# A four-layer graph network on one core: two groups' recurrences in alternate steps, and states brought back to rows by block turns and DRAM

## The chip, the cores and the metric

The kernel runs on one NeuronCore of one Trainium2 chip. The metric is device time in microseconds (us) of one launch. The time before is the median of three runs, 1408.24 us (1407.55 to 1408.32).

## What is computed

The input is `x` (128 graphs, 64 nodes, 256 features, float32) with an adjacency `adj` (128, 64, 64) of zeros and ones. Four layers follow each other; each takes `h = relu(layernorm(x))` and adds its result to `x`:

- layer 0: graph attention with four heads of 64 features; layer 1: graph attention with one head of 256 features;
- layer 2: a relational convolution; since `adj` holds only 0 and 1, only its loop relation counts;
- layer 3: a gated recurrence of three steps, which is where the change lies:

```python
for i in range(3):
    m = jnp.einsum('bnd,de->bne', h, weight[i])
    aggr = jnp.einsum('bst,bsd->btd', A, m)      # A = (adj != 0)
    gi, gh = aggr @ w_ih.T + b_ih, h @ w_hh.T + b_hh
    r, z = sigmoid(i_r + h_r), sigmoid(i_z + h_z)
    n = tanh(i_n + r * h_n)
    h = (1 - z) * n + z * h
```

## The kernel before

**Groups.** The 8192 node rows are cut into 16 groups of 512 rows (8 graphs, `G = 4` tiles of 128 rows). For each group the kernel runs layers 0 to 2 and then the recurrence. All matmuls are float32, and one product in the program is two passes in the trace (a transpose is one).

**How the order comes about.** The program does not issue its instructions as it is written. The class `Plan` notes every operation with the engine, a cost, the tiles it touches and a due time (`begin(name, start, end)`), then lays all of them on the five engines in its own model of time, and emits them in that order (`forward`, `backward`, `emit`, L316 to L472). Every engine then works through a fixed list, in order. The due times are constants in the last part of the program: `start, period = 87.96, 83.9` places the recurrence of group `g` at `start + g * period`, and layers 0 to 2 of later groups are placed ahead of it, so that their work fills the recurrence's waits. Since nearly all noted operations go through one helper, they all carry its line, L485; the small products of `beside` carry L706.

**One step of the recurrence** (`recurrence`, from L855). A state lives turned, as `hT` (features on partitions, 512 nodes along). A step has two chunks of 128 output features (`Chunk`). A chunk forms the gates r and z by a seven-product scheme (`mul`, products 1 to 7, with sums of states `hS`, `aS` made on GpSimd by `state_sums`) in the PSUM tiles `ry`, `rm`, `rz`, and the candidate in `nh`, `ni`. ScalarE copies the partial sums out of `ry` three times per chunk while it is still being added to; VectorE and ScalarE do the gates; the last two VectorE operations (`h_there`) write the new `hT`.

**The sum over neighbours** (`along`) needs the state as rows, `hnat` (nodes on partitions). It multiplies 64 by 64 blocks, four at a time in the four quarters of the array (`beside`, L706), into PSUM tiles `tp` and `tq`, from which ScalarE writes `aT`. The rows come from `back`: four TensorE transposes per 128 features into `tp`, and a ScalarE copy to `hnat`, or, after the third step, a VectorE addition of `x`. So a step has eight transposes. In the second and third steps `along` is issued in two halves, one per 128 features, so that the first can begin before the second chunk of the state is there:

```python
along(psum, hnat, abd, aT, [0])      # 16 products 64x64, then state_sums(aT, aS, 0)
...
back(hT, hnat, 1)                    # 4 transposes and a copy
along(psum, hnat, abd, aT, [1])
```

**Groups in time.** The three steps of one group follow each other directly, and then come the three of the next: a step's first products need the state that the step before has just finished.

**PSUM.** [...] `Banks` gives one each to `ry`, `rm`, `rz`, `nh` and `ni`, and three (`mt`) to everything else. **Transfers.** All but the first few DMAs are issued from one queue, that of SyncE (SP), in the planned order; from group 2 on, layers 0 to 2 and the start of the recurrence turn their input by a VectorE block turn (`nc.vector.transpose`, 32 by 32 blocks) and 16 small DMAs (`hT<-hn`) that move the blocks to their places (`layernorm_T_by_dma`).

Of the kernel before, what the change touches and what calls it, by code (L numbers as in the profile page):

```python
# [195 lines left out]
class Op:  # L196
    def __init__(self, engine, call, cost, port, dma, job, number):
        self.engine, self.call, self.cost, self.port, self.dma = engine, call, cost, port, dma
        self.job, self.number = job, number
        self.after, self.then, self.bases, self.needs = {}, [], [], []  # L200

# [18 lines left out]
class Plan:  # L220
# [60 lines left out]
    ISSUE = 665.0  # L281
# [34 lines left out]
    def forward(self):  # L316
# [11 lines left out]
        wire = 2500.0  # L328
# [29 lines left out]
        while len(order) < len(self.ops):  # L358
# [31 lines left out]
            if op.dma:  # L390
                wire = max(wire, t + 1350.0) + op.cost
                op.end = wire + 400.0
            else:
                took = op.cost
                if op.port:
                    other = "Pool" if e == "DVE" else "DVE"
                    took = max(took, held[other] + min(op.port, took) - t)
                    held[e] = t + took
                op.end = t + took + (165.0 if e == "PE" else 0.0)
                free[e] = t + took - (op.cost - op.busy)  # L400
# [118 lines left out]
def cost(engine, method, args, kwargs):  # L519

    n = elements(args[0])
    if engine == "tensor":
        m = elements(args[2] if method == "matmul" else args[0])
        return max(m / 1.2, 118.0) * (1 if method == "transpose" else 2)
# [17 lines left out]
def kernel(  # L542
# [62 lines left out]

    def pair(hT, k, s):
# [3 lines left out]
    def layernorm_T(work, psum, src, hT, natural=None, graphs=False):  # L610
# [28 lines left out]
        if natural is not None:  # L639
            nc.vector.tensor_scalar(natural, hn, 0.0, None, op0=ALU.max)  # L640

    def layernorm_T_by_dma(work, src, hT, natural=None, graphs=False):
# [14 lines left out]
        for p in range(n):  # L657
            nc.scalar.activation(hn[:, p, :], src[:, p, :], AF.Relu, bias=var[:, p : p + 1], scale=rstd[:, p : p + 1])
        tb = work.tile([P, K, n, P], F32, name="tb")
        nc.vector.transpose(tb.rearrange("p k n q -> p n k q"), hn.rearrange("p n (k q) -> p n k q", k=K))  # L660
# [10 lines left out]
    def transpose_blocks(psum, dst, src, rblocks, scale=1.0):  # L671

        for k in range(K):
            for r0 in range(0, rblocks, 4):
# [4 lines left out]
                nc.scalar.mul(dst[:, k, r0 * P : (r0 + n) * P], pt[:, : n * P], scale)  # L679
# [20 lines left out]
    def beside(products, cost):  # L700
# [10 lines left out]
        nc.note("PE", emit, cost, [Plan.all_of(x) for x in writes], [x for p in products for x in p[1:]])  # L711
# [61 lines left out]
    def aggregate_graphs(work, psum, t, wv, heads, by_scalar=False):  # L773
# [5 lines left out]
        for u in range(n // 2):  # L779
# [8 lines left out]
            beside(products, 710.0 if heads > 1 else 660.0)  # L788
# [11 lines left out]
    def along(psum, hnat, abd, aT, cs):  # L800
# [3 lines left out]
        for i, c in enumerate(cs):  # L804
            for p in range(G):
                for half, ps in enumerate(banks):
                    b = slice(half * N, (half + 1) * N)
                    for f in range(0, P, N):
                        products.append((ps[f : f + N, i, p, :], hnat[b, p, c * P + f : c * P + f + N], abd[b, p, :]))
        beside(products, 230.0 + 480.0 * len(cs))  # L810
# [29 lines left out]
    def before_recurrence(work, psum, src, adjacency, abd, by_dma=False):  # L840

        hT = work.tile([P, K, T], F32, name="hT")
        hnat = work.tile([P, G, D], F32, name="hnat")
# [5 lines left out]
        aT = work.tile([P, K, T], F32, name="aT")  # L849
        along(psum, hnat, abd, aT, range(K))  # L850
        hS = work.tile([P, 4, T // 2], F32, name="hS")
        aS = work.tile([P, 4, T // 2], F32, name="aS")
        for k in range(K):
            state_sums(hT, hS, k)
            state_sums(aT, aS, k)  # L855
        return hT, aT, hS, aS

    def recurrence(work, psum, start, src, abd, store, in_parts=False):

        hT, aT, hS, aS = start  # L860

        def back(hT, hnat, c, plus=None, p0=0, n=G):

            pt = psum.tile([P, n, P], F32, name="tp")
            for p in range(n):
                nc.tensor.transpose(pt[:, p, :], hT[:, c, (p0 + p) * P : (p0 + p + 1) * P], ident)
            part = (slice(None), slice(p0, p0 + n), slice(c * P, (c + 1) * P))
            if plus is None:
                nc.scalar.copy(hnat[part], pt)
            else:  # L870
                nc.vector.tensor_tensor(hnat[part], pt, plus[part], ALU.add)
                if in_parts:
                    store(hnat, part)

        class Chunk:
# [3 lines left out]
            def __init__(self, c, i, hT, hnew):  # L879
                self.c, self.i, self.hT, self.hnew = c, i, hT, hnew  # L880
                self.banks, self.started = {}, set()
                self.r, self.t, self.z, self.d = (work.tile([P, T], F32, name=name) for name in "rtzd")

            def bank(self, name):

                if name in self.banks:
                    return self.banks[name], False
                self.banks[name] = psum.tile([P, T], F32, name=name)
                return self.banks[name], True

            def mul(self, name, q, source):

                w, m, ms = ((whh, self.hT, hS), (wc[:, self.i], aT, aS))[source]
                ws = wsum[:, (0, 1 + self.i)[source]]
                cs = slice(self.c * P, (self.c + 1) * P)
                zs = slice(D + self.c * P, D + (self.c + 1) * P)
                lhsT, rhs = {
                    1: (w[:, 0, cs], m[:, 0, S0]),
                    2: (w[:, 1, cs], m[:, 1, S0]),
                    3: (ws[:, 2, cs], m[:, 1, S1]),  # L900
                    4: (w[:, 1, zs], ms[:, 3]),
                    5: (ws[:, 0, cs], ms[:, 0]),
                    6: (ws[:, 1, cs], ms[:, 1]),
                    7: (w[:, 0, zs], ms[:, 2]),
                }[q]
                ps, new = self.bank(name)
                nc.tensor.matmul(
                    ps[:, S0], lhsT, rhs, start=new, stop=(source == 1 and q in (2, 3, 4)), skip_group_check=True
                )
                return 0.43  # L910

            def both(self, name, q):
                return self.mul(name, q, 0) + self.mul(name, q, 1)

            def gate(self, name, k):

                w, m = {"nh": (whh, self.hT), "ni": (wc[:, self.i], aT)}[name]
                ps, new = self.bank(name)
                f = 2 * D + self.c * P
                nc.tensor.matmul(ps, w[:, k, f : f + P], m[:, k, :], start=new, stop=not new)  # L920
                return 0.86

            def nh_there(self):
                nc.scalar.activation(self.t, self.banks["nh"], AF.Identity, bias=bh[:, 4 + self.c : 5 + self.c])

            def r_there(self, h):

                r, t = self.r[:, h], self.t[:, h]
                if h == S0:
                    nc.vector.tensor_tensor(r, self.banks["rm"][:, S0], r, ALU.add)  # L930
                    y = r
                else:
                    y = self.banks["ry"][:, S0]
                nc.scalar.activation(r, y, AF.Tanh, bias=brz[:, self.c : self.c + 1], scale=0.5)
                nc.vector.scalar_tensor_tensor(t, r, 1.0, t, op0=ALU.add, op1=ALU.mult)

            def n_there(self, h):
                t = self.t[:, h]
                nc.vector.tensor_tensor(t, t, self.banks["ni"][:, h], ALU.add)
                nc.scalar.activation(t, t, AF.Tanh, bias=bi[:, 4 + self.c : 5 + self.c])  # L940
                nc.gpsimd.tensor_tensor(self.d[:, h], self.hT[:, self.c, h], t, ALU.subtract)

            def m1_there(self):
                nc.scalar.copy(self.r[:, S0], self.banks["ry"][:, S0])

            def m16_there(self):
                nc.scalar.copy(self.z[:, S0], self.banks["ry"][:, S0])

            def m165_there(self):
                nc.scalar.copy(self.z[:, S1], self.banks["ry"][:, S0])  # L950

            def z_there(self, h):

                z = self.z[:, h]
                nc.vector.tensor_tensor(z, self.banks["rz"][:, S0], z, ALU.add)
                nc.scalar.activation(z, z, AF.Tanh, bias=brz[:, 2 + self.c : 3 + self.c], scale=0.5)

            def h_there(self, h):
                d = self.d[:, h]
                nc.vector.scalar_tensor_tensor(d, self.z[:, h], 1.0, d, op0=ALU.add, op1=ALU.mult)  # L960
                nc.vector.scalar_tensor_tensor(
                    self.hnew[:, self.c, h], d, 0.5, self.t[:, h], op0=ALU.mult, op1=ALU.add
                )

        for i in range(LAYERS):
            last = i == LAYERS - 1
# [5 lines left out]
            if i > 0:  # L972
                aT = work.tile([P, K, T], F32, name="aT")
                if 0:
                    back(hT, hnat, 1)
                    along(psum, hnat, abd, aT, range(K))
                else:
                    along(psum, hnat, abd, aT, [0])
                state_sums(aT, aS, 0)
# [3 lines left out]
            if i > 0 and not 0:  # L983
                back(hT, hnat, 1)
            a.gate("nh", 1)
            a.nh_there()
            if i > 0:
                if not 0:
                    along(psum, hnat, abd, aT, [1])
                state_sums(aT, aS, 1)  # L990
# [34 lines left out]
            hnat = work.tile([P, G, D], F32, name="hnat")  # L1025
            back(hnew, hnat, 0, src if last else None)
# [618 lines left out]
```

## Time and profile before

| what | us |
|---|---|
| median of three runs | 1408.24 |
| the profiled execution's own time | 1407.86 |
| its span, first to last instruction | 1406.1 |
| TensorE (PE) busy | 1390.5 |
| VectorE (DVE) busy | 1026.9 |
| ScalarE (ACT) busy | 811.0 |
| GpSimd (POOL) busy | 609.7 |

The profile is of one execution. A group's "busy" is the time in which at least one of its instructions was running; for matmuls the ends are modelled and overlap, so the pitch, from the start of one to the start of the next, is what a product takes of TensorE. In a timeline line the columns are the start and the duration in us, engine, line, operation, output<-inputs, the part of the array used, shape and count; what stands in brackets at the end is idle time and what ended it.

### The profile page before, as it was taken

The numbers are of one execution on the slowest core, as the hardware profiler recorded it, in microseconds if no ns is written. First come the engines' busy times: TensorE is split into PE (matmuls) and PEld (weight loads), VectorE is DVE, ScalarE is ACT, GpSimd is POOL, SyncE is SP. The second block draws the span as 40 slices with busy tenths as digits, with TensorE's granted clock in tenths as the row PEclk, the third lists the DMA queues.
The fourth block names the chain that finished last, engine by engine and source line by source line (L and its number), as shares of the span: only waits on it lengthen the run. The fifth ranks groups of instructions, "written<-read, shape, count | busy, mean of one in ns | idle before, by whom it ended". The sixth has DMA issues, their size and how long they took to land.

```text
span 1406.1 us, 27921 instructions
## 1 busy us (share of the span) xinstructions
PE 1390.5 (99%) x9651; PEld 962.1 (68%) x9651; DVE 1026.9 (73%) x2553; ACT 811.0 (58%) x2045; POOL 609.7 (43%) x744
## 2 busy tenths in 40 slices
PE   9999999999999999999999999999999999999997
PEld 8676666767667676766767666676767767676775
DVE  5676787895858779586876859778686978765544
ACT  4765665556565655656665555656646565564543
POOL 2443444445444444543445445434543544452432
PEclk9999999999999999999999999999999999999999
DMA  7100222222222122222312222231222222111000
GB/s 194 51 16 21 40 68 38 51 54 49 60 50 67 33 50 52 50 61 41 81 33 51 48 51 63 39 76 26 47 43 52 49 36 47 40 24 31 16 16 18
DMA packets 299420, 67.89 MB, mean 48 GB/s; under 512 B 274696, under 2 KB 297480, under 8 KB 299272
## 3 DMA queue, kind: packets, MB, share of 16 engines
q1 hardware_dynamic: 298712, 65.50, 22.2%
q8 instruction: 80, 1.31, 0.4%
q14 instruction: 68, 0.56, 0.1%
q10 hardware_dynamic: 560, 0.52, 0.1%
HBM read 28.06 MB, written 8.53 MB: 26 GB/s over the span
## 4 chain that ended last, share of the span: by engine, by line
PE 91%; DVE 3%; SPq 2%; ACT 1%; POOL 1%; DMA 1%; issue 0%; DVEq 0%; POOLq 0%
PE ry L485 23%; PE mm L485 15%; PE rz L485 12%; PE ni L485 11%; PE nh L485 11%; PE rm L485 6%; PE tp L485 4%; PE mm L706 3%; PE tp L706 3%; SPq L485 2%; PE ni L1427 1%; DVE d L485 1%; DMA t<-row 1%; PE tq L706 1%; ACT hn L485 0%
## 5 line engine op out<-in xcount | busy, mean ns | idle before, releaser
L485 POOL TENSOR_TENSOR d<-hT,t 128x256 f32<-128x256 f32 x192 | 150.8, 794 | 453.3 <-ACT t L485 448.3
L485 PE MATMUL nh<-hT,whh 128*128 128x512 f32 x384 | 196.9, 597 | 0.0
L485 PE MATMUL ni<-aT,wc 128*128 128x512 f32 x384 | 196.8, 596 | 0.0
L485 ACT COPY z<-ry 128x256 f32<-128x256 f32 x192 | 71.0, 370 | 156.6 <-PE ry L485 123.1
L485 POOL TENSOR_TENSOR hS<-hT 128x256 f32<-128x256 f32 x96 | 77.9, 812 | 143.8 <-PE ry L485 95.4
L485 DVE SCALAR_TENSOR_TENSOR d<-z,d 128x256 f32<-128x256 f32 x192 | 119.3, 644 | 22.2 <-POOL d L485 10.6
L485 ACT ACTIVATE z<-z,brz 128x256 f32<-128x256 f32 x192 | 97.3, 507 | 66.0 <-DVE z L485 65.4
L485 DVE SCALAR_TENSOR_TENSOR t<-r,t 128x256 f32<-128x256 f32 x192 | 92.0, 480 | 55.9 <-ACT r L485 46.9
L485 ACT ACTIVATE hn<-xg,var,rstd 128x256 f32<-128x256 f32 x200 | 106.5, 592 | 22.2 <-DVE var L485 22.0
L485 DVE TENSOR_TENSOR z<-rz,z 128x256 f32<-128x256 f32 x192 | 80.3, 418 | 52.1 <-PE rz L485 31.8
L485 PE MATMUL rz<-hS,whh 128*128 128x256 f32 x384 | 116.6, 385 | 0.1
L485 PE MATMUL ry<-hS,wsum 128*128 128x256 f32 x384 | 116.4, 385 | 0.2
L485 PE MATMUL mm<-wl,hT 128*128 128x512 f32 x248 | 116.3, 595 | 0.0
L485 PE MATMUL rz<-aS,wc 128*128 128x256 f32 x384 | 115.3, 382 | 0.0
L485 PE MATMUL ry<-aS,wsum 128*128 128x256 f32 x384 | 114.3, 379 | 0.0
L485 ACT ACTIVATE t<-t,bi 128x256 f32<-128x256 f32 x192 | 93.7, 504 | 33.1 <-DVE t L485 31.0
L485 DVE SCALAR_TENSOR_TENSOR hT<-d,t 128x256 f32<-128x256 f32 x192 | 102.9, 558 | 2.5
L485 PEld LDWEIGHTS ry<-hS,wsum 128*128 128x128 f32 x384 | 70.0, 190 | 42.2 <-issue 23.1
L485 DVE BATCH_NORM_STATS2 st<-xg 128x6 f32<-128x256 f32 x256 | 94.3, 409 | 6.1 <-POOL xg L485 2.9
L485 PEld LDWEIGHTS rz<-hS,whh 128*128 128x128 f32 x384 | 69.1, 190 | 38.7 <-issue 25.3
L485 POOL TENSOR_TENSOR rstd<-var,mhalf 128x4 f32<-128x4 f32 (+1 forms) x70 | 69.9, 999 | 56.3 <-DVE var L485 54.0
L485 POOL TENSOR_TENSOR aS<-aT,aS 128x256 f32<-128x256 f32 x96 | 72.1, 752 | 43.8 <-ACT aT L485 43.0
(205 smaller groups left out, 3234.7 us busy)
## 6 DMA issues: line engine op xcount, KB each, us to landing
hT<-hn SPq DMA_DIRECT2D x896, 32.0 KB, 1.9
xg<-in_x_dram SPq DMA_DIRECT2D x15, 512.0 KB, 5.6
out_dram<-hnat SPq DMA_DIRECT2D x15, 512.0 KB, 3.3
t<-row SPq DMA_DIRECT2D x28, 256.0 KB, 3.5
at<-in_adj_dram SPq DMA_DIRECT2D x64, 32.0 KB, 2.2
eg<-in_adj_dram SPq DMA_DIRECT2D x64, 32.0 KB, 2.2
ag<-in_adj_dram SPq DMA_DIRECT2D x16, 128.0 KB, 2.5
t<-row SPq DMA_DIRECT2D x28, 64.0 KB, 2.8
```

Source lines behind the costliest of these rows:

```text
L485: return do(*[real(a) for a in args], **{k: real(v) for k, v in kwargs.items()})
L706: nc.nc.tensor.matmul(*[real(x) for x in product], start=True, stop=True)
L1427: nc.spare = lambda: psum.spare and nc.nc.tensor.matmul(pause, warm, warm, start=True, stop=True)
```

## The change

**The states' way back.** In 45 of 48 steps the eight transposes go. `back_by_dma` turns 32 by 32 blocks of each half of the state on VectorE, writes the result to a DRAM tile in one transfer of 512 KB, and reads it back in four transfers of 128 KB, one for each 32 partitions, so that the rows arrive in place:

```python
def back_by_dma(self, dram):
    tb = self.work.tile([P, P // S, G, K, S], F32, name="tb")
    for c in range(K):
        nc.vector.transpose(tb[:, :, :, c].rearrange("p j n b -> p n j b"),
                            self.hT[:, c, :].rearrange("p (n j a) -> p n j a", n=G, a=S))
    turned = dram.tile([P, P // S, G * K * S], F32, name="turned")
    nc.sync.dma_start(turned, tb.rearrange("p j n k b -> p j (n k b)"))
    self.hnat = self.work.tile([P, D // N, G, N], F32, name="hnat")
    for j in range(P // S):
        nc.sync.dma_start(self.hnat[j * S : (j + 1) * S].rearrange("p i n b -> p i (n b)"),
                          turned[:, j].rearrange("(i a) x -> a i x", a=S))
```

The order of features inside `hnat` is now another one (`spread`); the weights that meet it are laid out to match (`turned=True`). After a third step, `finish` adds the rows to `x` on GpSimd and the output is stored from there. The old way stays for the first step of group 0 and the last two steps of group 15.

**Alternate steps.** The recurrence becomes a class with `ahead` (one whole `along`, and the sums), `step` and `back_by_dma`, and the steps of two groups take turns, each in a slot of 27.0:

```diff
-        start, period = 87.96, 83.9
+        start, slot = 87.96, 27.0
+        steps = [(0, 0), (0, 1)]
+        for g in range(1, NG):
+            steps += [(g, 0), (g - 1, 2), (g, 1)]
+        steps.append((NG - 1, 2))
...
+        for n, (g, i) in enumerate(steps):
...
+            if n == 0 or steps[n - 1] != (g, i - 1):
+                nc.begin(("ahead", g, i), at - 14.0, at)
+                running[g].ahead()
...
+            nc.begin(("step", g, i), at, at + slot)
...
+            running[g].step(i, quick or final, final)
+            if not (quick or final):
+                nc.begin(("back", g, i), at + slot, at + 1.5 * slot)
+                running[g].back_by_dma(dram)
+                if i == LAYERS - 1:
+                    running.pop(g).finish()
```

`along` is always whole now (`range(K)`), never in halves. The due times of layers 0 to 2 are moved to suit; group 1 is to be ready 30 earlier by them.

**PSUM and buffers.**

```diff
-            own = ("ry", "rm", "rz", "nh", "ni")
+            own = ("ry", "rz", "nh", "ni")
...
-                return 3 if tag == "mt" else 1
+                return {"mt": 4, "ry": 1, "rz": 1}.get(tag, 1)
...
+                def half(self, name):
+                    ps, new = self.bank("ry" if name == "rm" else name)
+                    return ps[:, S1 if name == "rm" else S0], new
...
-                self.r, self.t, self.z, self.d = (work.tile([P, T], F32, name=name) for name in "rtzd")
+                self.r, self.t, self.z = (work.tile([P, T], F32, name=name) for name in "rtz")
+                self.d = self.r
...
-        W.append(Layer(3, gru, {"hT": 3, "hnat": 2, "aT": 2, "hS": 2, "aS": 2}))
+        W.append(Recurrent(3, gru, {"hT": 4, "hnat": 2, "aT": 2, "hS": 2, "aS": 2, "r": 2, "t": 2, "z": 2}))
```

`rm` moves into the second half of the bank of `ry`, and the bank so freed goes to the other work (`mt`). `r`, `t` and `z` get two buffers each, and `d` takes the place of `r`.

**The planner's own costs.** The modelled price of a TensorE product changes a little, and two `beside` groups in succession are priced lower (`TURN`), so that the planner likes to put them side by side.

## The prediction

> **What bounds the kernel now.** I read the page first: busy time by engine, then the chain that ended last.
>
> ```profile
> PE 1390.5 (99%) x9651; PEld 962.1 (68%) x9651; DVE 1026.9 (73%) x2553; ACT 811.0 (58%) x2045; POOL 609.7 (43%) x744
> PE 91%; DVE 3%; SPq 2%; ACT 1%; POOL 1%; DMA 1%; issue 0%; DVEq 0%; POOLq 0%
> ```
>
> TensorE (PE) is busy 99% of the span and makes 91% of the chain, so what counts is how much its list holds and how long it waits. Busy says nothing of the first, since products overlap in it; the pitch does, from the timeline of TensorE's products:
>
> ```profile
> 699.94 0.60 PE L485 MATMUL tp<-ident,hT 128*128 128x128 f32 x4
> 700.38 1.02 PE L485 MATMUL ni<-aT,wc 128*128 128x512 f32 x2
> ...
> 702.53 0.59 PE L485 MATMUL rz<-aS,wc 128*128 128x256 f32 x2
> 703.06 0.27 PE L706 MATMUL tp<-abd,hnat 64*64 64x64 f32 x2
> ...
> 703.53 0.22 PE L706 MATMUL tq<-abd,hnat 64*64 64x64 f32 x2
> 703.68 1.12 PE L485 MATMUL nh<-hT,whh 128*128 128x512 f32 x2
> ```
>
> Four transposes take 0.44 us until the next product starts: 0.11 each. A product of 512 columns takes 0.86, one of 256 takes 0.43. The product at 702.53 is therefore through at 702.96, and a half `along` (16 products of 64x64) takes from there to 703.68: 0.72. A whole one:
>
> ```profile
> 738.02 0.60 PE L485 MATMUL ry<-hT,whh 128*128 128x256 f32 x2
> 738.55 0.27 PE L706 MATMUL tp<-abd,hnat 64*64 64x64 f32 x2
> ...
> 739.49 0.23 PE L706 MATMUL tq<-abd,hnat 64*64 64x64 f32 x2
> 739.64 0.70 PE L485 MATMUL ry<-aT,wc 128*128 128x256 f32 x2
> ```
>
> From 738.45 to 739.64: 1.19, for twice the products. Two halves are 1.44, so going into the 64x64 form and out again costs 0.25 beside the products.
>
> With these pitches I summed TensorE's list of before, from the first `along` (at 85.49 in the trace) to the last transpose (at 1399.76): 1291.6 us of products and passages in 1314.3 us. Only 22.7 us are waits. The list, then, sets the time, to within 2%.
>
> **What the Trainium skill says.** "TensorEngine Tiling (Array Packing)", Tiling Modes, Key Properties: changing the tiling mode drains TensorE. The 0.25 us agrees. "VectorE: DVE Perf Modes", The three transpose paths: VectorE turns 32x32 blocks only, into SBUF, TensorE a whole 128x128 into PSUM; hence the transfers that put the blocks in place. "DMA: Bandwidth & Descriptors", Two DMAs through the same engine are not ordered: the reading transfer has to wait until the writing one has landed. The trace has this pattern in `row<-fT` and `t<-row`: SyncE waited 14 times, 15.0 us in all. "SBUF — State Buffer", SBUF: two separate sides: VectorE with two SBUF inputs and GpSimd hold one port pair in turns. The trace agrees: near the end the same `hT<-d,t` took 0.92 us beside a GpSimd operation and 0.42 without.
>
> **The change, part by part.** Rows for what goes and comes:
>
> ```profile
> L485 PE MATMUL tp<-ident,hT 128*128 128x128 f32 x384 | 61.4, 275 | 3.1 <-DVE hT L485 3.1
> L485 DVE STREAM_TRANSPOSE hn<-hnat 128x1024 f32<-128x1024 f32 x14 | 17.4, 1242 | 12.4 <-ACT hnat L485 8.2 <-DMA hT<-hn 3.4 <-ACT es L485 0.7
> L485 DVE TENSOR_TENSOR hnat<-tp,xg 128x512 f32<-128x512 f32 x31 | 21.1, 683 | 4.9 <-PE tp L485 4.7
> L485 ACT COPY hnat<-tp 128x512 f32<-128x512 f32 x64 | 37.4, 584 | 25.4 <-PE tp L485 24.9
> L485 POOL TENSOR_TENSOR xg<-xg,hn 128x1024 f32<-128x1024 f32 x28 | 69.8, 2494 | 13.5 <-DVE hn L485 13.5
> ```
>
> *Transposes.* 45 of 48 steps lose eight: 360 x 0.11 = 39.6 us off TensorE. (By the busy column it would be 61.4/384 = 0.16 each, 57.6; that counts overlap, so I take the pitch.)
>
> *Passages into the 64x64 form.* The instruction order of the changed kernel, as built, has 106 runs of 64x64 products where the one before has 160. 32 fewer come from the joined halves, 22 from groups put side by side. 54 x 0.25 = 13.5 us.
>
> *TensorE together*: -53.1 us. Nothing is added to its list in the steady part. Before the first `along` the new list is 1.8 us longer (ten more warming products, a little of group 1's work); TensorE has 18 us of idle or waiting there (85.49 against 67.5 us of listed work), which hides it; uncovered it would cost 1.8.
>
> *VectorE.* 90 turns of 512 elements: between half of 1242 (621 ns) and the 683 of a same-sized addition; I take 650: +58.5. Thirty additions of 683 go: -20.5. Net +38 us, beside TensorE. In the steady stretch from 669 to 1088 VectorE was busy 321.6 of 419.0 us (77%); that is five groups of 16, so with 5/16 of the 38 more in 5/16 of 53 less it is 83%. `d` in `r`'s place moves no work.
>
> *ScalarE* loses 60 copies (35 us), and 128 copies of 256 become 64 of 512. *GpSimd* gains 15 additions at 2494 ns: +37 us, to 48%; each can hold VectorE's port, or stand ahead of the sums `aS` that a step waits for, for up to 2.5 us. Both ends of that: 0, and 37 if each one is met; I take it with the waits below.
>
> *SyncE and DMA.* 225 more issues. A `hT<-hn` burst shows the price of one:
>
> ```profile
> 717.80 21.11 SPq L485 DMA_DIRECT2D hT<-hn  x31
> ...
> 742.14 10.72 SPq L485 DMA_DIRECT2D hT<-hn  x15
> out_dram<-hnat SPq DMA_DIRECT2D x15, 512.0 KB, 3.3
> ag<-in_adj_dram SPq DMA_DIRECT2D x16, 128.0 KB, 2.5
> ```
>
> 0.68 us each: +153 us on SyncE, which also stands still while `turned` lands. Everything queued behind it (layer inputs, `t<-row`, the bursts) moves back by a few us; layers have slack by their due times, since 51.3 are given to each.
>
> *The return's length and its cover.* Last product to finished `hT` was 3.5 us at the end of the trace (1396.2 to 1399.7); second turn 0.65; `turned` 3.3 (the row of the other 512 KB store); four issues 2.7; landing 2.5 (the 128 KB row): 12.7 us. The traces of before don't show these two transfers, so from both sides: 9 if the issues overlap the landing, 20 if the reads with their 1 KB pieces take double. In the new order TensorE has, between a step's last product and the `along` that needs its rows, 18 to 32 us of other products by the pitches, 25 in the middle (30 returns are followed by an `along`). That is the other group's step; it hides the return. If the cover is gone, each late return costs its excess on TensorE.
>
> *Waits.* A step no longer waits for its predecessor's last state; of before's 22.7 us such waits are about 5 (2.54 and 1.77 are the longest). On the other side VectorE's idle share falls from 23 to 17%; if the waits grow as it shrinks, 22.7 x 23/17 is 8 more. `ry` and `rm` in one bank: chunk b's first product must follow chunk a's last reading. The listed distance between the two is 2.6 us in the middle (2.2 before), at the least 0 once and 0.86 else; reading takes 0.47 (`r<-ry`) and the handing over, so this is a microsecond or two in all. Net +3; ends -8 and +20.
>
> *Sum* on the profiled execution: 1406.1 - 53.1 + 3 = 1356.0 span; 1.8 lie around it (1407.9 - 1406.1): 1357.8; the median is 0.4 above the profiled one: **1358**.
>
> **Rivals.**
> 1. *The list shrinks, but VectorE becomes a second bound.* For it: 83% busy, GpSimd on the same port, and three ScalarE copies per chunk in `ry`'s chain. Against: 73% gave only 22.7 us of waits. At 0.3 us of wait per chunk, 96 chunks give 29 us: some 1384. Its span is 1367 to 1400.
> 2. *Slower: rows come late, behind SyncE's bursts.* The four reads stand in one list with bursts of 16 `hT<-hn` (10.7 us); two bursts between `turned` and its reads are 21.1 us, so the return takes 33.8 against 25 of cover: 8.8 late, and TensorE stands. It decides from 53/30 = 1.8 us per return on. Ten returns so placed: 88 us, 1358 + 88 = 1446. Against: in the new order there is seldom more than half a burst between the two.
> 3. *No change*: the transposes filled waits that remain. For it: little; waits are 22.7 us in all, half of the saving, so this needs new waits of 50 by chance: 1408.
>
> **How the numbers follow.** Forecast (1347 to 1366) 0.66; rival 1 0.22; rival 2 0.07; rival 3 0.03; below 1347 (all waits but ten gone) 0.02. A range of 1347 to 1378 holds the first and 0.14 of the second. Faster 0.66 + 0.22 + 0.02 = 0.90, same 0.03, slower 0.07; 0.2% (2.8 us) is about what a measurement of this kernel can tell from no change.
>
> **What would show it.** `tp<-ident,hT` x24, pitch unchanged, and TensorE's busy time near 1340. The whole `along` at 1.19. `turned` landing near 3.3, `hnat<-turned` near 2.5. Few waits of `tp<-abd,hnat` for `DMA hnat`; many would be rival 2. Waits of `ry` and `rz` products for VectorE or ScalarE adding up to 30 us would be rival 1. I am wrong if TensorE's idle exceeds 60 us.

## The result, and the profile after

The changed kernel takes 1418.4 us (median of four runs, 1416.4 to 1421.0) where the kernel before takes 1408.3 beside it: a ratio of 1.0074, 95% interval 1.0056 to 1.0091. It is slower by 0.7%; the forecast was 1358. The profiled execution took 1418.6 with a span of 1416.8.

The busy line and the chain of the changed kernel's page:

```profile
PE 1361.1 (96%) x9311; PEld 923.7 (65%) x9311; DVE 1047.4 (74%) x2627; ACT 778.8 (55%) x1921; POOL 655.8 (46%) x759
PE 77%; DVE 10%; ACT 4%; SPq 4%; POOL 2%; issue 2%; DMA 1%; DVEq 0%; ACTq 0%; POOLq 0%
```

TensorE has 340 recorded instructions fewer, and its share of the chain fell from 91% to 77%: VectorE and ScalarE now end waits that hold it. The transfers and turns came near their prices. Groups with their counts, busy time, mean ns and idle time before, then two rows of DMA issues with the us to landing:

```profile
L489 PE MATMUL tp<-ident,hT 128*128 128x128 f32 x24 | 4.1, 282 | 7.8 <-DVE hT L489 7.8
L489 DVE STREAM_TRANSPOSE tb<-hT 128x512 f32<-128x512 f32 x90 | 62.4, 699 | 4.0 <-DMA hT<-tb 3.1
L489 POOL TENSOR_TENSOR xg<-xg,hnat 128x1024 f32<-128x1024 f32 x15 | 36.2, 2415 | 0.0
turned<-tb SPq DMA_DIRECT2D x45, 512.0 KB, 3.2
hnat<-turned SPq DMA_DIRECT2D x180, 128.0 KB, 2.8
```

**A ledger of TensorE.** In the timeline of its products I summed every pitch (start to next start) from 85 us on and sorted it in three: transposes of states, products in the 64x64 form (with passages), and all the rest. The few warming products (`ni<-warm`, 0.4 and 1.1 us) are left out. The rest then holds the same products in every kernel here, so what it grows by is waits, and products that run slower.

| us, from 85 us on | before | after | difference | forecast |
|---|---|---|---|---|
| transposes `tp<-ident,hT` | 43.7 | 3.3 | -40.4 | -39.6 |
| products in the 64x64 form | 110.9 | 101.6 | -9.3 | -13.5 |
| the rest | 1159.9 | 1218.6 | +58.6 | +3 |
| together | 1314.5 | 1323.5 | +9.0 | -50.1 |

The span grew by 10.7, so the ledger explains all but 1.7 of it. Of the 53.1 us forecast to be saved, 49.7 arrived, and 58.6 us of new waits and slower products took them.

**A part that is not waits.** In two stretches, 120.9 to 124.3 and 998.1 to 1005.0 us, the clock granted to TensorE was 0.5 of full speed; the kernel before has no such stretch that lies between 85 us and its last product. In the second one:

```profile
1001.11 3.62 PE L489 MATMUL nh<-hT,whh 128*128 128x512 f32 x4
1004.52 0.82 PE L489 MATMUL ry<-hT,whh 128*128 128x256 f32 x2
```

These four passes of 512 columns take 3.41 us until the next product starts, where the prediction's pitch (0.86 for two) gives 1.72. TensorE was busy 9.1 of the 10.3 us, so I estimate the loss at half of that, 4.6 of the 58.6 us. Both stretches begin beside waits: in the 4 us ahead of them TensorE was busy 2.55 and 1.95 us. So it is in all 33 such stretches of the traces here (18 to 64% busy in the 4 us ahead, against 96 to 99% of whole spans): a wait of TensorE can cost more than its own length. How long a wait has to be for that is not measured.

Where are the waits? TensorE's named waits of the changed kernel (those for which the profile tells what ended them), the five largest, with total us, times and longest us:

```profile
PE ry L489 <- DVE r L489: 15.5, 28, 0.7
PE tp L489 <- DVE hT L489: 7.8, 4, 2.5
PE ry L489 <- ACT z L489: 5.3, 10, 1.0
PE ry L489 <- ACT r L489: 5.3, 9, 1.1
PE ry L489 <- DMA hT<-tb: 5.0, 2, 3.2
```

The kernel before had nothing of the first kind but this:

```profile
PE rm L485 <- DVE r L485: 0.6, 2, 0.3
```

No product of an `along` waits for `DMA hnat`: the rows are in time. What is new are short waits of `ry` products. One chunk of the changed kernel, all engines (lines of other work left out):

```profile
847.13 0.59 PE L489 MATMUL ry<-hT,whh 128*128 128x256 f32 x2
...
847.76 0.37 ACT L489 COPY r<-ry 128x256 f32<-128x256 f32 x1 [0.70 <-PE ry L489]
...
848.19 0.70 PE L489 MATMUL ry<-aT,wc 128*128 128x256 f32 x2 [0.46 <-ACT r L489]
...
848.72 0.59 PE L489 MATMUL ry<-hS,wsum 128*128 128x256 f32 x2
...
849.43 0.42 DVE L489 TENSOR_TENSOR r<-ry,r 128x256 f32<-128x256 f32 x1 [1.67 <-PE ry L489]
...
850.00 0.67 PE L489 MATMUL ry<-aS,wsum 128*128 128x256 f32 x2 [0.68 <-DVE r L489]
```

ScalarE at 847.76 reads the first half of the bank; the second-half product at 848.19 waits until it is done. VectorE at 849.43 reads the second half (the old `rm`), the only thing it ever reads there; the first-half product at 850.00 waits until it is done. Neither pair touches a common element. `Plan` notes halves, so it laid the list out as if these waits did not exist, and TensorE meets them in mid-chunk with nothing else to do. The Trainium skill, "PSUM — Partial Sum Buffer", PSUM bank collisions raise a hardware error, says why such a wait must stand: two engines may not be in one bank and quadrant (32 partitions) at once, reads included, and a guard goes by bank and quadrant, not by address. The runs here show the waits alone.

### The profile page after: what moved, and what is told of

Read it like the earlier page. It is cut to its first block, busy times and chain, and to the rows that moved or that the text cites. A ratio compares the mean times of both kernels' runs of the same rounds, so it can differ in the third digit from the quotient of the medians.

```text
span 1416.8 us, 27135 instructions
## 1 busy us (share of the span) xinstructions
PE 1361.1 (96%) x9311; PEld 923.7 (65%) x9311; DVE 1047.4 (74%) x2627; ACT 778.8 (55%) x1921; POOL 655.8 (46%) x759
## 4 chain that ended last, share of the span: by engine, by line
PE 77%; DVE 10%; ACT 4%; SPq 4%; POOL 2%; issue 2%; DMA 1%; DVEq 0%; ACTq 0%; POOLq 0%
PE ry L489 27%; PE mm L489 14%; PE nh L489 10%; PE ni L489 9%; PE rz L489 9%; SPq L489 4%; DVE r L489 2%; PE mm L730 2%; PE tp L730 2%; DVE t L489 2%; ACT hn L489 2%; ACT z L489 1%; DVE hn L489 1%; PE ni L1541 1%; PE tp L489 1%
## 5 line engine op out<-in xcount | busy, mean ns | idle before, releaser
L489 POOL TENSOR_TENSOR r<-hT,t 128x256 f32<-128x256 f32 x192 | 148.9, 785 | 354.6 <-ACT t L489 354.2
L489 POOL TENSOR_TENSOR aS<-aT 128x256 f32<-128x256 f32 x96 | 77.3, 805 | 133.4 <-ACT aT L489 133.3
L489 DVE SCALAR_TENSOR_TENSOR t<-r,t 128x256 f32<-128x256 f32 x192 | 100.3, 526 | 41.4 <-ACT r L489 36.1
L489 DVE SCALAR_TENSOR_TENSOR r<-z,r 128x256 f32<-128x256 f32 x192 | 110.7, 586 | 23.6 <-POOL r L489 15.8
L489 PE MATMUL ry<-aT,wc 128*128 128x256 f32 x384 | 115.0, 387 | 6.2 <-ACT r L489 3.1
L489 PE MATMUL ry<-hT,whh 128*128 128x256 f32 x384 | 111.1, 391 | 8.8 <-DMA hT<-tb 5.0
L489 ACT ACTIVATE hn<-xg,var,rstd 128x256 f32<-128x256 f32 x200 | 106.0, 592 | 10.8 <-DVE var L489 10.2
L489 DVE SCALAR_TENSOR_TENSOR hT<-r,t 128x256 f32<-128x256 f32 x192 | 102.4, 549 | 1.5
```

The source lines that it names most:

```text
L489: return do(*[real(a) for a in args], **{k: real(v) for k, v in kwargs.items()})
```

## The experiments

Theory A: the shared `ry`/`rm` bank, with an order that doesn't know of it, makes the waits. Theory B: VectorE's load, late rows, SyncE's queue, or the alternation. All runs are against the kernel before on the same chip. "Rest" is the ledger's third row less the 1159.9 of before; "half clock" is the length of the stretches between 85 us and the last product in which the granted clock was 0.5 (at most half of it is lost); "r waits" are TensorE's named waits for VectorE's `r`. These three are of the profiled execution, in us. "Laid out again" is explained at the end of this section.

| kernel | median us | ratio, 95% interval | rest | half clock | r waits |
|---|---|---|---|---|---|
| *return by TensorE* | | | | | |
| before, laid out again | 1415.2 | 1.0048 (1.0032 to 1.0065) | +3.7 | 6.8 | none |
| before, bank shared | 1440.1 | 1.0224 (1.0207 to 1.0242) | +32.2 | 0 | 12.4 |
| before, shared, order told | 1414.1 | 1.0043 (1.0026 to 1.0060) | +6.9 | 6.8 | 3.5 |
| alternate, own bank | 1410.7 | 1.0018 (1.0009 to 1.0027) | +4.2 | 3.4 | none |
| alternate, shared | 1430.3 | 1.0151 (1.0134 to 1.0168) | +25.9 | 0 | 14.3 |
| *return through DRAM* | | | | | |
| after (shared) | 1418.4 | 1.0074 (1.0056 to 1.0091) | +58.6 | 10.2 | 15.5 |
| after, laid out again | 1393.7 | 0.9892 (0.9875 to 0.9910) | +30.7 | 0 | 8.6 |
| own bank | 1389.0 | 0.9872 (0.9830 to 0.9914) | +24.1 | 0 | 0.3 |
| own bank, laid out again | 1406.2 | 0.9992 (0.9984 to 1.0001) | +26.4 | 17.1 | none |
| own bank, no turns | 1395.7 | 0.9909 (0.9893 to 0.9926) | +30.5 | 17.1 | none |
| own bank, ScalarE's queue | 1394.9 | 0.9902 (0.9885 to 0.9918) | +30.0 | 10.2 | none |
| own bank, no return | 1379.8 | 0.9791 (0.9775 to 0.9807) | +16.4 | 6.8 | none |
| order told | 1390.1 | 0.9874 (0.9858 to 0.9891) | +22.2 | 6.8 | 2.7 |
| order told, laid out again | 1402.6 | 0.9956 (0.9939 to 0.9972) | +29.5 | 10.2 | 4.8 |
| two `ry` tiles | 1395.2 | 0.9909 (0.9892 to 0.9925) | +26.5 | 10.2 | 3.1 |
| `rm` with `rz` | 1397.0 | 0.9912 (0.9895 to 0.9929) | +29.2 | 17.1 | 9.3 |
| `rm` with `rz`, told | 1379.7 | 0.9801 (0.9782 to 0.9820) | +12.8 | 0 | 2.4 |
| the same, laid out again | 1380.2 | 0.9797 (0.9781 to 0.9813) | +15.4 | 3.4 | 0.8 |
| the same, rows by ScalarE | 1388.6 | 0.9865 (0.9849 to 0.9882) | +14.2 | 3.4 | 1.7 |

### The bank and the return, each alone

`rm` gets its bank back in the changed kernel (e1):

```diff
-own = ("ry", "rz", "nh", "ni")          # mt 4
+own = ("ry", "rm", "rz", "nh", "ni")    # mt 3
-ps, new = self.bank("ry" if name == "rm" else name)
-return ps[:, S1 if name == "rm" else S0], new
+ps, new = self.bank(name)
+return ps[:, S0], new
```

> The changed kernel with one part undone: the rm products have a PSUM bank of their own again and the bank pool has 3 buffers again instead of 4. Alternate steps, VectorE turns and transfers through DRAM stay. The listed work of TensorE is 6 us above that of the changed kernel. Theory A (the shared ry/rm bank: each product into one half waits for the readers of the other half, which the order was not laid out for; 60 of the about 57 to 65 us of added waits): the waits fall back to those of the kernel before, 1360 us, range 1350 to 1375; the wait of ry products for VectorE's r disappears. Theory B (load of VectorE and GpSimd, late rows or the alternation itself make the waits): 1405 to 1425, little moved. Between, 1375 to 1405: both have a share.

The reverse in the kernel before (e2): `own` without `rm`, `mt` 4, `half` and `begun` as in the change.

> The kernel before with one part of the change alone: rm in the second half of ry's bank, the pool with 4 buffers. No alternation, no return through DRAM. Theory A: the same new waits without the saving: 1408 plus 40 to 65, 1450 to 1475 us. Theory B: 1400 to 1415.

The changed kernel with TensorE's return in every step, shared (e3) and with `rm`'s own bank (e4):

```diff
-running[g].step(i, quick or final, final)
-if not (quick or final): ... running[g].back_by_dma(dram) ...
+running[g].step(i, True, final)
```

> The changed kernel with the return by TensorE in every step (transposes and ScalarE copies, the addition of the input in the last step on VectorE) and none through DRAM; the alternation and the shared bank stay. TensorE's listed work is 41 us above that of the changed kernel. Theory A: the waits stay, 1418 plus 35 to 45, 1450 to 1465 us. Theory B in the form late rows or the VectorE load of the turns: the waits go with the turns, 1418 plus 41 minus about 55, 1395 to 1410 us.

> Both undone: rm in its own bank, return by TensorE in every step. What stays of the change is the alternation of two groups, the layout of the rows, the tiles r/t/z doubled with d in r. TensorE's listed work is 6 us below that of the kernel before. Theory A: 1395 to 1410 us, as the kernel before or slightly under. If the alternation itself makes waits (a form of B): 1430 to 1470 us, as the shared one with TensorE's return.

Measured: 1389, 1440, 1430, 1411. Sharing alone costs the kernel before 2.24% (31.6 us), and the alternating one 19.5 us (1430.3 - 1410.7). One row of the page tells it, `ry<-aS,wsum` with its idle time at the end: in the kernel before, in it with the bank shared, in the changed kernel, and in that with the own bank.

```profile
L485 PE MATMUL ry<-aS,wsum 128*128 128x256 f32 x384 | 114.3, 379 | 0.0
L485 PE MATMUL ry<-aS,wsum 128*128 128x256 f32 x384 | 116.7, 385 | 4.7 <-DVE r L485 4.7
L489 PE MATMUL ry<-aS,wsum 128*128 128x256 f32 x384 | 116.5, 385 | 12.6 <-DVE r L489 12.0
L489 PE MATMUL ry<-aS,wsum 128*128 128x256 f32 x384 | 114.6, 380 | 0.0
```

Theory A holds in sign in all four, but not in size: 1389 lies between the two theories' ranges, and so do 1440 (for 1450 to 1475 under A) and 1430 (for 1450 to 1465). The 1411 is at the edge of A's 1395 to 1410: the alternation does little (1.0018, with a list of TensorE that is 6 us shorter), and that form of B falls. In e3 the bank is still shared, yet the rest is +25.9 for +58.6: a sign that the bank alone did not make all of the changed kernel's waits.

### Is it the bank, or the order that doesn't know of it?

The bank stays shared, but `Plan.note` takes every access to a `ry` tile as one to the whole tile, so that the order is laid out with the waits that TensorE meets. In the changed kernel (e6) and in the kernel before with the bank shared (e15):

```diff
 op = Op(engine, call, cost, port, dma, self.job, len(self.ops))
+whole = lambda v: self.all_of(v) if v.base.tag == "ry" and v.base.pool.psum else v
+writes, reads = [whole(v) for v in writes], [whole(v) for v in reads]
```

> The changed kernel, its bank still shared, but the order is laid out with the whole ry tile as one region: a product into one half is placed after the readers of the other half, as TensorE then waits in fact. TensorE's listed work is 1 us above the changed kernel's. Theory A1 (the loss is that the order does not know of the waits, so that TensorE meets them with nothing else to do): most of the 29 us come back, 1390 to 1400. Theory A2 (the shared bank is in itself too short of room, whatever the order): 1412 to 1425.

> The kernel before with rm in ry's bank and 4 pool buffers (1440 us), and the order told that the whole ry tile is one region. If what the shared bank costs is the order's ignorance of the waits (A1), the 32 us go here too: 1405 to 1416. If the changed kernel's recovery with the order told came from something else: 1425 to 1445.

Measured 1390.1 and 1414.1: 28 us back in one, 26 in the other, in both the range of A1 (the 28 loses weight below, where the orders are laid out again). In the kernel before, the row above with the bank shared and the order told:

```profile
L487 PE MATMUL ry<-aS,wsum 128*128 128x256 f32 x384 | 114.3, 379 | 0.0
```

None of this row's idle time is left, with the bank as shared as it was; the named waits for VectorE's `r` fell from 12.4 to 3.5 us. Then other places for `rm`: two `ry` tiles with `mt` 3 (e9), `rm` in the second half of `rz`'s bank (e10), and that with the order told (e13: the edit above with `"rz"`):

```diff
-return {"mt": 4, "ry": 1, "rz": 1}.get(tag, 1)
+return {"mt": 3, "ry": 2, "rz": 1}.get(tag, 1)      # e9
-ps, new = self.bank("ry" if name == "rm" else name)
+ps, new = self.bank("rz" if name == "rm" else name)  # e10, e13
```

> The changed kernel with two ry tiles (each still with rm in its second half) and 3 pool buffers. The products of the next chunk can begin while the last readers of this one are out; the waits inside a chunk for the readers of the other half stay. TensorE's listed work is 7 us above the changed kernel's. If the waits are those inside a chunk: 1405 to 1420. If they are between chunks: 1385 to 1397.

> The changed kernel with rm in the second half of rz's bank in the place of ry's; ry has its bank alone, the pool keeps 4. Each rz tile has two readers, each ry tile four, so fewer pairs of product and reader meet. Theory A with the number of readers deciding: 1395 to 1408, between the own bank (1389) and the shared (1418). If any sharing costs the same: 1412 to 1425.

> The changed kernel with rm in rz's bank and 4 pool buffers (1397 us), and the order told that the whole rz tile is one region. TensorE's list is 4 us above the changed kernel's. If the order's knowledge of the waits is what counts: 1385 to 1391, as with ry's bank told (1390) and the own bank (1389). If the place of rm counts beside it: 1393 to 1400.

Measured 1395.2, 1397.0 and 1379.7. Two tiles fell in the range foreseen for waits between chunks, though their waits inside a chunk stay; with orders scattering as shown below, that does not decide where in a chunk the waits arise. With `rz`, the waits for VectorE's `r` moved to `rz` products (9.3 us) and fell when the order was told (2.4). The last is below both its ranges, and it is 2.0% faster than the kernel before, the fastest complete kernel of the study:

```profile
PE 1346.9 (98%) x9339; PEld 928.3 (67%) x9339; DVE 1069.1 (78%) x2627; ACT 774.8 (56%) x1921; POOL 664.3 (48%) x759
```

VectorE is busier than in the changed kernel (78 to 74%), and TensorE waits less: a sign against VectorE's load as the cause of the waits.

### What the other 20 us are not

From the own-bank kernel: the turns left out (e8), the return's 225 transfers issued by ScalarE (e11), the whole return left out (e12). From `rm` with `rz`, told: the attention's 84 row transfers issued by ScalarE (e14).

```diff
-nc.sync.dma_start(turned, tb.rearrange(...))    # e8: and no nc.vector.transpose
+nc.sync.dma_start(turned, self.hT.rearrange("p k t -> p (k t)").rearrange(...))
-nc.sync.dma_start(self.hnat[...], turned[...])  # e11, turned too
+nc.scalar.dma_start(self.hnat[...], turned[...])
-running[g].back_by_dma(dram)                    # e12
-nc.sync.dma_start(row..., fT...)                # e14, t<-row too
+nc.scalar.dma_start(row..., fT...)
```

> The kernel with rm's own bank (1389 us), without the 90 VectorE turns of the return: the transfer out reads hT itself, so that the rows come back unturned and the output is not the reference's. VectorE has 90 times 0.65 = 58 us less, the return is 1.3 us shorter at each half turned. All transfers stay. If VectorE's load makes the waits that are left against the return by TensorE (about 16 us): 1370 to 1380. If late rows, SyncE's queue or the alternation make them: 1384 to 1392.

> The kernel with rm's own bank (1389 us), the 225 transfers of the return issued by ScalarE in the place of SyncE. If SyncE's queue, on which a transfer waits behind others that are not ready (hT<-tb late by 2 to 7 us in all), is the cause of the rest: 1375 to 1384. If not, ScalarE's added issues cost something: 1389 to 1400.

> The kernel with rm's own bank (1389 us), with no return at all after 45 of the 48 steps: no turns, no transfers, and the next step's along (and the addition of the input) reads the group's old rows, so the output is not the reference's. TensorE's list is the same to 1 us. It is the floor of what a return through DRAM can reach. If the 20 us of waits that the own-bank kernel has above the one with TensorE's return come from the return (its turns on VectorE, its 225 transfers in SyncE's queue, rows that are late): 1365 to 1373. If they come from TensorE's list itself, which has 40 us less work to put between the products that wait: 1382 to 1392.

> The kernel with rm in rz's bank and the order told (1380 us), the 84 transfers of the attention rows (row<-fT and two t<-row for each) issued by ScalarE in the place of SyncE, so that they do not stand behind a burst of 16 hT<-tb issues. If SyncE's queue makes the waits that are left (DMA and DVE t, about 10 us of the list): 1368 to 1375. If not: 1377 to 1388.

Measured 1395.7, 1394.9, 1379.8 and 1388.6: three of the four lie outside both ranges named for them, and only e11's is in one (SyncE's queue not the cause). Less work on VectorE or SyncE bought nothing, so neither is shown to be the cause, and neither is excluded by one order each; without any return the rest is still +16.4. SyncE's bursts do make single waits, though of another kind than I had feared. In the changed kernel, SyncE's issues and then TensorE's products:

```profile
984.04 1.19 SPq L489 DMA_DIRECT2D t<-row  x2
985.27 1.30 SPq L489 DMA_DIRECT2D hT<-hn  x2
986.69 10.85 SPq L489 DMA_DIRECT2D hT<-tb  x16
```

```profile
995.77 0.27 PE L489 MATMUL tp<-ident,fs 128*16 128x128 f32 x1
999.27 1.19 PE L489 MATMUL ry<-hT,whh 128*128 128x256 f32 x2 [3.22 <-DMA hT<-tb]
```

The 16 blocks of a new group's first state leave SyncE by 997.5, and the step that needs them has been ready before: 3.2 us, the longest wait of the steady part, and the clock of 0.5 from 998.1 on doubles the price of what follows (1.19 us for the two passes). It is the next group's input that is late, not a returned row.

### How much is the order itself?

Every edit makes `Plan` lay out all five lists anew. So five kernels were laid out a second time with nothing altered but one estimate:

```diff
-LATENCY = 170.8
+LATENCY = 175.0
```

> The kernel with rm's own bank (1389 us), its order laid out again with a latency estimate of 175.0 in the place of 170.8 ns and nothing else altered: how far the time moves by the order alone. If differences of 6 to 9 us between kernels of one kind (no turns 1396, returns on ScalarE's queue 1395, no return 1380) can be put to their edits: within 3 of 1389. If they are scatter of the order: 5 or more away, either side.

> The kernel with rm in rz's bank and the order told (1380 us), its order laid out again with a latency estimate of 175.0 ns. If the place of rm in rz's bank is worth 10 us beside the order's knowledge: 1376 to 1384. If its 10 us are scatter of the order: up to 1390.

> The kernel before, its order laid out again with a latency estimate of 175.0 in the place of 170.8 ns. The scatter of its order: with TensorE waiting 10 us in all beside the passages, little room to get better: 1405 to 1415. If its order is a lucky one as well: 1415 to 1430.

> The changed kernel, its order laid out again with a latency estimate of 175.0 ns. If the shared bank that the order doesn't know of makes the loss: 1410 to 1430, with 15 to 22 us of TensorE's waits named for VectorE's r again. If 1418 was an unlucky order: 1390 to 1405.

> The changed kernel with the order told of the whole ry tile (1390 us), laid out again with a latency estimate of 175.0 ns. If the order's knowledge is worth the 28 us: 1383 to 1397, and waits for VectorE's r under 6 us. If that was scatter: up to 1406, as the own bank laid out again.

First order against second: own bank 1389.0 and 1406.2, `rm` with `rz` told 1379.7 and 1380.2, before 1408.3 and 1415.2, after 1418.4 and 1393.7, told 1390.1 and 1402.6. The changed kernel itself, with 4 ns more in one estimate, is faster than the kernel before by 1.1%: that is the range foreseen for an unlucky first order (1390 to 1405), and the waits for VectorE's `r` are 8.6 us, not the 15 to 22 of a loss that is all the bank's. The second times of the told order (1402.6) and of the own bank (1406.2) too are what was foreseen for scatter, that of the kernel before lies on the line between its two ranges, and only `rm` with `rz`, told, kept its time. In the own bank's second order nine named waits of 11.0 us stand directly behind products in the 64x64 form (in the ledger's second row, so not in "rest"), and 8.2 of them are for `hT<-tb`, a new group's input; this is the longest:

```profile
742.95 0.67 PE L489 MATMUL ry<-hT,whh 128*128 128x256 f32 x2 [2.31 <-DMA hT<-tb]
```

In each pair the slower order has more time at half clock: 10.2 us against 0 in the changed kernel, 17.1 against 0 with the own bank. At half their length, the most they can cost, these make 5 of 25 and 8.5 of 17 us. The clock also scatters from launch to launch: the own bank's four took 1385.2 to 1398.0 us at mean clocks of 0.998 to 0.991.

So a difference under some 25 us between two kernels with the DRAM return, one order each, cannot be put to its edit: not the 28 of e6 with certainty either (over two orders each, shared, told and own bank average 1406, 1396 and 1398), nor e8, e9, e10, e11, e12 and e14 among each other. The kernels with TensorE's return scatter less (rest 0, +3.7 and +4.2 for three with an own bank), and against that the shared bank's +32.2 and +25.9, and +6.9 told, stand out clearly, though each of these is one order.

## Why the prediction was wrong, step by step

- *Transposes, -39.6*: right, -40.4. *Passages, -13.5*: -9.3, somewhat too much; the 0.25 came from one pair of places.
- *VectorE's, GpSimd's and the transfers' prices*: a block turn 699 ns for 650, the addition 2415 for 2494, `turned` 3.2 us for 3.3, `hnat` 2.8 for 2.5. Sound. VectorE's 83% in the steady stretch was not: it was 313.3 of 419.0 us, 75%, for the list did not get shorter in time, and VectorE's total rose by 20.5 and not by 38.
- *The return is hidden by 18 to 32 us of cover*: right, no `along` waited for its rows. Rival 2 as priced did not occur.
- *"`ry` and `rm` in one bank ... a microsecond or two in all"*: this step failed. I priced one place, the first product of chunk b behind the last reading of chunk a. And the microsecond or two never entered the sum: "Net +3" is the +8 and the -5 alone. Inside a chunk three ScalarE copies and one VectorE addition read the bank while products go into its other half, and 28 of these meetings, in 96 chunks, became waits for VectorE alone. 15.5 us are named for VectorE's `r`, and part of the 10.6 for ScalarE's `r` and `z`, which copy out of `ry` in every version. In the kernels with TensorE's return the sharing cost 31.6 and 19.5 us.
- *"Net +3; ends -8 and +20"* for the waits: this failed more widely. The rest grew by 58.6, and even without the sharing by 24.1 and 26.4. Some 4.6 of the 58.6 are products at half clock, for which the prediction had no term; and its upper end of +20 left out the 37 that it had set for GpSimd. I had taken waits of before (22.7 us) as a property of the kernel; they belong to one laid-out order, in which TensorE's list is the longest of the five. With 50 us less in it, lateness of any engine shows. That last sentence is argued, not shown: the +16.4 without any return speaks for it, in one order alone, and what would prove it was not tried.
- *Rival 1's sign* ("waits of `ry` and `rz` products for VectorE or ScalarE adding up to 30 us") appeared, 26.1 us, but nothing shows VectorE's load as its cause: the own bank left 0.3 us and none of the waits for VectorE's `r`, in two orders with VectorE at 77 and 75%, busier than the 74% of the changed kernel. The sign did not tell the two apart.
- *The side*: slower is true of this order. The same source's second order is 1.1% faster than before, and still 36 us above the forecast. So the forecast of "faster" failed partly by the luck of one order, while its size failed in every order. That the shared bank, unknown to the order, costs 20 to 30 us is shown where orders scatter little; how the remaining +13 to +31 of the other DRAM-return kernels divide stays open.

## What to carry to other kernels

Two tiles in one PSUM bank are one tile to every wait: count each pair of product and reader across the halves, not only the hand-over at the end, and if a planner lays out the lists, tell it of the waits that TensorE will meet (26 us here, in the kernel before with the bank shared, for two lines of code). Where an engine has been filled to 99%, work taken off it is worth its price only if the waits stay where they were, so estimate them anew and keep a wide end. And lay the same kernel out twice before a difference is put to an edit: here one estimate moved by 4 ns was worth up to 25 us. Look at the granted clock too when two kernels are compared.

## What was not expected of the hardware

The waits across the halves are short and alike: 28 of them, 0.55 us in the mean and 0.7 at most, about VectorE's reading (0.42) and a hand-over (0.15 in the chunk shown). And VectorE's share says little of who waits for it: the fastest kernel has it at 78%, the changed one, with over four times the growth of the ledger's rest (58.6 to 12.8), at 74%. And in 33 places of the traces a stretch in which TensorE had little to do is followed by 3.4 or some 6.8 us at half clock, which the list of waits doesn't show.
